# Issuing the routed experts' first token loads behind the shared expert's last load

## The chip, the cores and the metric

The kernel runs on one core of one Trainium2 chip. The core has five engines that run side by side and meet only at semaphores: TensorE (PE in the profile; its weight loads are the row PEld), VectorE (DVE), ScalarE (ACT), GpSimd (POOL) and SyncE (SP). Transfers are started by instructions on SP, ACT or POOL; "SPq" in a row is the queue of transfer instructions that SP works through. The metric is the device time of one execution in microseconds (us), as a median over runs.

## The reference

The computation is four layers in sequence, each one normalizing its input and adding its result to it, on 8 sequences of 512 tokens with 256 channels:

```python
x = x + _L0_attn_ref(_layernorm(x), ...)   # gated recurrence and an MLP
x = x + _L0_ffn_ref(_layernorm(x), ...)    # mixture of experts
x = x + _L1_attn_ref(_layernorm(x), ...)   # gated delta rule
x = x + _L1_ffn_ref(_layernorm(x), ...)    # attention over chosen tokens
```

The change lies in the second layer. Every token goes through one shared expert and through 2 of 8 routed experts, which a softmax over 8 scores picks:

```python
_, idx = jax.lax.top_k(scores + gate_b, 2)
weights = jnp.take_along_axis(scores, idx, axis=-1)
...
h = swiglu((xt @ ew1 + eb1) * (xt @ ew3 + eb3))      # 256 -> 1024 -> 512
acc + ce[:, None] * (h @ ew2 + eb2)                  # 512 -> 256, weighted
...
shared = swiglu((xt @ sw1 + sb1) * (xt @ sw3 + sb3)) @ sw2 + sb2
return (routed + shared)
```

## The kernel before, in words

The four layers are four functions that are traced one after the other: `first_block` (L241), `experts` (L418), `delta_rule` (L566) and `chosen_attention` (L1100). Activations pass between layers through DRAM, in one buffer `xbuf` for each sequence. All arithmetic is in fp32.

`first_block` also routes: for each sequence it leaves the normalized tokens in SBUF (`bz`, eight tiles that stay) and the two chosen experts of every token. `places` (L207) then works out for every token and choice a row of a DRAM buffer `zbuf`, in which tokens of one expert lie together in tiles of 128 rows; there are 71 such tiles.

`experts` has two parts.

**Shared part**, one turn for each of the 8 sequences. `scatter(b)` (L494) issues eight indirect transfers on POOL (L499), each of which writes 128 normalized tokens to their rows of `zbuf`; 64 in all. `shared(b)` (L479) loads the sequence's activations from `xbuf` into the tile `sx` (L481, on SP), turns the normalized tokens with eight transposes (L122), multiplies by the shared weights (L444: 64 matmuls of 128x512), runs the swiglu on ACT and DVE (L448 to L462), adds the bias of the second product to `sx` (L485, on DVE, one instruction), multiplies by the second weights (L490: 32 matmuls), adds that to `sx` (L491) and stores `sx` back to `xbuf` (L492, on SP). There are two `sx` tiles, so the load of sequence n+2 can only follow the store of sequence n.

**Routed part**, one turn for each of the 71 tiles. `fetch(k)` (L504) gathers the tile's expert weights `w` (L508, an indirect transfer on POOL, three buffers), loads its 128 tokens from `zbuf` into `zt` (L510, on SP, three buffers), and turns them (L513, L515). `hidden` and `results` do the matmuls (L444 with the tile `p_r`, L522), and the result is stored to `ybuf` (L525, on SP).

A load of `zt` reads rows of `zbuf` that any scatter may have written, so it waits until the last of the 64 scatters has landed.

The order of the instructions on each engine is not the order of the source. A scheduler puts each engine's instructions into a fixed sequence when the kernel is built, earliest first by its own estimate of when each is ready; on the chip every queue is worked through in that sequence, and an instruction that waits holds up what follows on the same queue. `tc.issue_after(ins)` puts what is traced inside the block behind `ins` in that sequence, for instructions on the same engine as `ins`; it adds no wait for `ins` to finish. The helper `behind` (L527) uses it to put a step of one tile behind the last matmul of the step before. That instruction is on PE, so it orders PE's work alone and says nothing of the loads on SP.

In the kernel before, the queue of SP through this stage reads, in order: store of sequence 2, load of sequence 4, store 3, load 5, the three `zt` loads of tiles 0, 1 and 2, store 4, load 6, store 5, load 7, store 6, the `zt` load of tile 3, store 7, the `zt` load of tile 4, and then stores of `ybuf` and loads of `zt` in turn.

DVE's sequence through this stage has a similar property: L485 of sequence n+1 stands in the middle of the turn of sequence n, between L459 and L449 of that turn.

Of the kernel before, what the change touches and what calls it, by code (L numbers as in the profile page):

```python
# [36 lines left out]
def bc(ap, axis, n):  # L37

    ap = ap.unsqueeze(axis)
    shape = list(ap.shape)  # L40
    shape[axis] = n
    return ap.to_broadcast(shape)
# [3 lines left out]
def block(ctx: ExitStack, tc: tile.TileContext, a: dict, out: bass.AP):  # L46
    nc = tc.nc
# [40 lines left out]
    zbuf = dram.tile([NTILES * TILE, D], F32, name="zbuf")  # L88
    ybuf = dram.tile([NTILES * TILE, D], F32, name="ybuf")

    xbufs = [[dram.tile([T, D], F32, name=f"xbuf{n}_{b}") for b in range(B)] for n in range(2)]


    def rows_of(buf):
        return buf.rearrange("(t p) d -> p t d", p=P)
# [21 lines left out]
    def turn(pool, tag, src, dst, n, weight=None):  # L117

        for c in range(DK):
            pt = pool.tile([P, T], F32, name=f"pt{n}_{c}", tag=tag)  # L120
            for t in range(NT):
                TE.transpose(pt[:, t * P : (t + 1) * P], src[:, t, c * P : (c + 1) * P], ident)  # L122
            if weight is None:
                S.copy(dst[:, c, :], pt)
            else:
                S.activation(dst[:, c, :], pt, AF.Copy, scale=weight[:, c : c + 1])  # L126
# [291 lines left out]
    def experts():  # L418
# [3 lines left out]
        with ExitStack() as cx:  # L422
# [40 lines left out]
                yield  # L463
                return hT

            last_of, hidden_of = [None], [None]

            def whole(gen):

                while True:  # L470
                    try:
                        next(gen)
                    except StopIteration as e:
                        return e.value

            def second(w):
                return w[:, 2 * DK * I2 : WMAT].rearrange("p (f d) -> p f d", d=D)

            def shared(b):  # L479
                x = ch.tile([P, NT, D], F32, name=f"sx{b}", tag="sx")  # L480
                nc.sync.dma_start(x, rows_of(xbufs[0][b]))  # L481
                xT = ch.tile([P, DK, T], F32, name=f"sxT{b}", tag="xT")
                turn(pm, "p1", zs[b], xT, f"s{b}")
                hT = whole(hidden(xT, shared_w, T, f"s{b}"))
                V.tensor_add(x, x, bc(shared_w[:, WMAT + 16 :], 1, NT))  # L485
                w2 = second(shared_w)
                for t in range(NT):
                    ps = po.tile([P, D], F32, name=f"pys{b}_{t}", tag="po")
                    for f in range(4):
                        TE.matmul(ps, hT[:, f, t * P : (t + 1) * P], w2[:, f, :], start=f == 0, stop=f == 3)  # L490
                    V.tensor_add(x[:, t, :], ps, x[:, t, :])  # L491
                nc.sync.dma_start(rows_of(xbufs[0][b]), x)  # L492
# [8 lines left out]
            def tile_rows(buf, k):  # L501
                return buf[k * TILE : (k + 1) * TILE, :]

            def fetch(k):  # L504

                w = ew.tile([P, WROW], F32, name=f"w{k}", tag="w")
                at = bass.IndirectOffsetOnAxis(ap=wrow[:, k : k + 1], axis=0)
                G.indirect_dma_start(w, None, a["experts"].rearrange("e p f -> (e p) f"), at)  # L508
                zt = ch.tile([P, D], F32, name=f"zt{k}", tag="zt", bufs=3)
                nc.sync.dma_start(zt, tile_rows(zbuf, k))  # L510
                pt = po.tile([P, DK, TILE], F32, name=f"ptz{k}", tag="po")
                for c in range(DK):
                    last_of[0] = TE.transpose(pt[:, c, :], zt[:, c * P : (c + 1) * P], ident)  # L513
                zT = ch.tile([P, DK, TILE], F32, name=f"zT{k}", tag="zT")
                S.copy(zT, pt)  # L515
                return w, zT
# [18 lines left out]
            for b in range(B):  # L535
                scatter(b)
                shared(b)


            last_of[0] = None  # L540
            ahead, due = behind(fetch, 0), None
            for k in range(NTILES):
                w, zT = ahead
                work = hidden(zT, w, TILE, f"r{k}")
                next(work)
                for bank in range(4):
                    if bank == 1 and k > 0:

                        with tc.issue_after(hidden_of[0].ins):
                            behind(next, work)  # L550
                    elif bank < 3:
                        behind(next, work)
                    else:
                        hT = behind(whole, work)
                    if bank == 1 and due is not None:
                        behind(results, *due)
                    if bank == 2 and k + 1 < NTILES:
                        ahead = behind(fetch, k + 1)
                due = k, w, hT
            behind(results, *due)  # L560

    experts()
    early.close()

# [827 lines left out]
```

## Time and profile before

| what | value |
|---|---|
| median of 3 runs | 3373.59 us (3373.55 to 3381.02) |
| the profiled execution | 3381.53 us, its span 3379.8 us |
| PE busy over the span | 3018.4 us, 89% |
| DVE, ACT, POOL busy | 56%, 46%, 17% |
| shared part (PE from first to last matmul of it) | about 535 to 847 us |
| routed part | about 847 to 1505 us |
| mean granted clock of TensorE | 0.91 |

The span runs from the first to the last instruction of the profiled execution; its own time is 1.7 us more, and the profile is one execution, so times within it are summed against 3381.53 us and not against the median. Rows of the timeline give a start, a duration, the engine, the line, the operation, and in brackets how long the engine stood idle before it and what ended that. A row with the engine SPq is the short time in which SP issues a transfer, not the transfer.

### The profile page before, as it was taken

What the parts mean: (1) busy time and instruction counts of PE and PEld (TensorE: products, weight loads), DVE (VectorE), ACT (ScalarE), POOL (GpSimd) and SP (SyncE); (2) the same over time, 40 slices, a digit from 0 to 9 for tenths busy, and PEclk for the clock granted to TensorE, in tenths of its full rate; (3) what the DMA queues carried; (4) which work ended last, traced back from release to release, by engine and by line L of the source; (5) the groups of instructions that cost most, each with busy time, mean ns of one, the idle gap of its engine ahead of it and who ended that gap; (6) DMA issues with size and microseconds to landing.
All of it is one profiled execution on the core that took longest, in us unless ns stands there. A gap on an engine that the chain in (4) does not pass through costs nothing.

```text
span 3379.8 us, 59439 instructions
## 1 busy us (share of the span) xinstructions
PE 3018.4 (89%) x24662; PEld 2227.4 (66%) x24662; DVE 1900.5 (56%) x4415; ACT 1548.0 (46%) x2747; POOL 574.0 (17%) x629
## 2 busy tenths in 40 slices
PE   7999999979999999977899898898989999498887
PEld 3655555535999999973566666666666667365664
DVE  4555545534555555556467767767677664554432
ACT  3554442212333333325466666767666663233322
POOL 1000001320000111014122222312121110212111
PEclk8999998989999999998789898989989896698787
DMA  5000003220788888871000000000000000201111
GB/s 205 13 25 13 13 13 148 69 67 19 271 337 330 330 327 320 327 284 31 2 1 20 8 20 8 26 2 26 2 23 2 8 2 8 94 23 42 36 40 47
DMA packets 97133, 302.69 MB, mean 90 GB/s; under 512 B 12760, under 2 KB 79456, under 8 KB 87648
## 3 DMA queue, kind: packets, MB, share of 16 engines
q0 software_dynamic: 19440, 221.19, 17.4%
q1 hardware_dynamic: 68016, 68.44, 6.0%
q10 hardware_dynamic: 9408, 9.27, 0.8%
q8 instruction: 194, 3.18, 0.4%
q14 instruction: 75, 0.61, 0.1%
HBM read 248.79 MB, written 50.08 MB: 88 GB/s over the span
## 4 chain that ended last, share of the span: by engine, by line
PE 69%; DVE 12%; DMA 11%; issue 4%; ACT 2%; POOL 2%; SPq 0%; another core or an unknown queue 0%; ACTq 0%; POOLq 0%; DVEq 0%
PE p_r L444 13%; PE pc L681 8%; DMA zbuf<-bz,rows 5%; PE pp L304 3%; PE pk L746 3%; PE pj L399 3%; PE pyr L522 3%; PE pkq L950 3%; DMA w<-in_experts,wrow 2%; PE pf L394 2%; PE p_s L444 2%; PE py L1008 2%; PE st L1271 2%; PE pw L957 1%; DVE cy L685 1%
## 5 line engine op out<-in xcount | busy, mean ns | idle before, releaser
L444 PE MATMUL p_r<-zT,w 128*128 128x128 f32 x4544 | 533.0, 275 | 6.1 <-DMA w<-in_experts,wrow 5.5
L444 PEld LDWEIGHTS p_r<-zT,w 128*128 128x128 f32 x4544 | 525.0, 192 | 11.6 <-issue 7.1
L685 DVE SCALAR_TENSOR_TENSOR cy<-pc,conv,cy 128x509 f32<-128x509 f32 (+2 forms) x480 | 351.4, 740 | 139.7 <-ACT cy L683 134.6
L448 ACT ACTIVATE t_r<-p_r,w 128x128 f32<-128x128 f32 x568 | 170.9, 374 | 263.5 <-PE p_r L444 183.9
L444 PE MATMUL p_s<-sxT,shared_w 128*128 128x512 f32 x512 | 226.2, 603 | 22.1 <-DVE l_s L449 20.4
L444 PEld LDWEIGHTS p_s<-sxT,shared_w 128*128 128x128 f32 x512 | 98.1, 193 | 145.6 <-issue 106.3
L508 POOL DMA_INDIRECT w<-in_experts,wrow x71 | 66.8, 940 | 676.3 <-ACT sg_r L457 655.8
L449 DVE SCALAR_TENSOR_TENSOR l_r<-p_r,w,t_r 128x128 f32<-128x128 f32 x284 | 80.0, 344 | 175.7 <-PE p_r L444 175.7
L681 PE MATMUL pc<-cxT,wq 128*128 128x512 f32 x256 | 150.8, 714 | 15.0 <-DVE cy L685 12.9
L681 PE MATMUL pc<-cxT,wk 128*128 128x512 f32 x256 | 146.0, 665 | 6.1 <-DVE cy L685 3.7
L304 PE MATMUL pp<-hT,win 128*128 128x512 f32 x320 | 142.9, 598 | 0.2 <-ACT hT L126 0.2
L522 PE MATMUL pyr<-w,htr 128*128 128x256 f32 x568 | 136.0, 383 | 2.6 <-DVE htr L462 2.6
L683 ACT ACTIVATE cy<-pc,conv 128x512 f32<-128x512 f32 x160 | 108.4, 686 | 62.3 <-PE pc L681 61.0
L449 DVE SCALAR_TENSOR_TENSOR g_r<-p_r,w,t_r 128x128 f32<-128x128 f32 x284 | 79.9, 344 | 98.8 <-PE p_r L444 98.8
L746 PE MATMUL pk<-kq 128*128 128x256 f32 x512 | 130.2, 391 | 0.7 <-DVE NQ L748 0.4
L728 POOL TENSOR_TENSOR e<-le,g 128x512 f32<-128x512 f32 x64 | 66.3, 1042 | 364.2 <-DVE NQ L748 341.6
L748 DVE SCALAR_TENSOR_TENSOR NQ<-pk,nbk,e 128x256 f32<-128x256 f32 x256 | 110.0, 477 | 27.2 <-PE pk L746 26.8
L394 PE MATMUL pf<-hT,fc 128*128 128x512 f32 x256 | 121.5, 601 | 0.0
L457 ACT ACTIVATE sg_r<-g_r 128x512 f32<-128x512 f32 x71 | 44.8, 631 | 159.9 <-DVE g_r L455 159.9
L399 PE MATMUL pj<-pj,sT 128*128 128x256 f32 x512 | 113.1, 379 | 0.0
L522 PEld LDWEIGHTS pyr<-w,htr 128*128 128x128 f32 x568 | 103.6, 192 | 14.2 <-issue 2.7
L950 PEld LDWEIGHTS pkq<-state,kq 128*128 128x128 f32 x768 | 95.4, 197 | 24.2 <-DVE state L972 16.7
(393 smaller groups left out, 6179.0 us busy)
## 6 DMA issues: line engine op xcount, KB each, us to landing
zt<-zbuf SPq DMA_DIRECT2D x71, 128.0 KB
ybuf<-yt SPq DMA_DIRECT2D x71, 128.0 KB
zbuf<-zeros SPq DMA_DIRECT2D x11, 768.0 KB
x<-in_x SPq DMA_DIRECT2D x8, 512.0 KB
xbuf<-x SPq DMA_DIRECT2D x8, 512.0 KB
sx<-xbuf SPq DMA_DIRECT2D x8, 512.0 KB
xbuf<-sx SPq DMA_DIRECT2D x8, 512.0 KB
cx<-xbuf SPq DMA_DIRECT2D x8, 512.0 KB
```

The costliest lines, as they stand in the source:

```text
L304: TE.matmul(ps, win[:, k, m : m + P], hT[:, k, :], start=k == 0, stop=k == DK - 1)
L394: TE.matmul(ps, fc[:, k, f * P : (f + 1) * P], hT2[:, k, :], start=k == 0, stop=k == DK - 1)
L399: TE.matmul(ps, sT[:, f, t * P : (t + 1) * P], pj[:, f, :], start=f == 0, stop=f == 7)
L444: last_of[0] = TE.matmul(ps[:, f, :], wx[:, k, (f0 + f) * P : (f0 + f + 1) * P], xin[:, k, :], start=k == 0, stop=k == DK - 1)
L448: S.activation(t3[:, f, :], p3[:, f, :], AF.Identity, bias=b3[:, f0 + f : f0 + f + 1])
L449: V.scalar_tensor_tensor(t1[:, f, :], p1[:, f, :], b1[:, f0 + f : f0 + f + 1], t3[:, f, :], ALU.add, ALU.mult)
L522: last_of[0] = TE.matmul(ps, hT[:, f, :], w2[:, f, :], start=f == 0, stop=f == 3)
L681: TE.matmul(ps, w[:, k, n * P : (n + 1) * P], xT[:, k, :], start=k == 0, stop=k == DK - 1)
L685: V.scalar_tensor_tensor(y[:, j:], ps[:, : T - j], conv[:, at + n, 3 - j : 4 - j], y[:, j:], ALU.mult, ALU.add)
L746: TE.matmul(pk[:, j, :, :], kq[:, h + j, 0, ts], kq[:, h + j, :, ts], start=True, stop=True)
L748: V.scalar_tensor_tensor(NQ[:, :, t * HG + h + j, :], pk[:, j, :, :], s.nbk[:, t, h + j : h + j + 1], bc(e[:, h + j, :], 1, 2), ALU.mult, ...
L950: TE.matmul(ps[:, n, h, :], s.kq[:, h, n, ts], state[:, h, :], start=True, stop=True)
```

## The change

The load of `sx` in `shared` is remembered in `sx_of`, and the load of `zt` in `fetch` is traced inside `tc.issue_after` of the last one remembered, which, when `fetch` runs, is the load of sequence 7.

```diff
-            last_of, hidden_of = [None], [None]
+            last_of, hidden_of, sx_of = [None], [None], [None]
...
                 x = ch.tile([P, NT, D], F32, name=f"sx{b}", tag="sx")
-                nc.sync.dma_start(x, rows_of(xbufs[0][b]))
+                sx_of[0] = nc.sync.dma_start(x, rows_of(xbufs[0][b]))
...
                 zt = ch.tile([P, D], F32, name=f"zt{k}", tag="zt", bufs=3)
-                nc.sync.dma_start(zt, tile_rows(zbuf, k))
+
+                with tc.issue_after(sx_of[0].ins):
+                    nc.sync.dma_start(zt, tile_rows(zbuf, k))
```

In the built kernel the queue of SP then reads: store 3, load 5, store 4, load 6, store 5, load 7, the `zt` loads of tiles 0, 1 and 2, store 6, the `zt` load of tile 3, store 7, and so on as before. These three instructions are all that moves: the sequences of PE, DVE, ACT and POOL are the same, instruction by instruction, and so is the rest of SP's. No transfer is added or taken away, and none changes its size.

## Prediction

> **What bounds the kernel now.** PE is busy 89% of the span, and the chain that ended last is mostly PE, so the kernel is near PE's own work; what can be won is PE's idle time. I read the chain first:
>
> ```profile
> PE 69%; DVE 12%; DMA 11%; issue 4%; ACT 2%; POOL 2%; SPq 0%; another core or an unknown queue 0%; ACTq 0%; POOLq 0%; DVEq 0%
> PE p_r L444 13%; PE pc L681 8%; DMA zbuf<-bz,rows 5%; PE pp L304 3%; PE pk L746 3%; PE pj L399 3%; PE pyr L522 3%; PE pkq L950 3%; DMA w<-in_experts,wrow 2%; PE pf L394 2%; PE p_s L444 2%; PE py L1008 2%; PE st L1271 2%; PE pw L957 1%; DVE cy L685 1%
> ```
>
> The third entry is odd: the scatter to zbuf should feed nothing until the routed part begins, yet 5% of the span (some 170 us) runs through it. Something in the shared part waits for the scatters. The waits of SP and then of PE, over 450 to 1000 us, name both ends of it:
>
> ```profile
> SPq L510 <- DMA zbuf<-bz,rows: 58.7, 1, 58.7
> ...
> PE p_s L444 <- DVE l_s L449: 20.4, 1, 20.4
> ```
>
> SP stands once for 58.7 us at a zt load, for the last scatter; PE stands once for 20.4 us in the shared matmuls. The timeline joins them:
>
> ```profile
> 716.02 0.42 DVE L491 TENSOR_TENSOR sx<-pys,sx 128x256 f32<-128x256 f32 x1 [1.30 <-PE pys L490]
> 717.10 15.72 PE L444 MATMUL p_s<-sxT,shared_w 128*128 128x512 f32 x36 [0.24 <-ACT sxT L124]
> ...
> 722.81 0.69 DVE L459 TENSOR_TENSOR g_s<-g_s,sg_s 128x512 f32<-128x512 f32 x1 [0.69 <-ACT sg_s L457]
> ...
> 740.17 0.96 POOL L499 DMA_INDIRECT zbuf<-bz,rows  x1 [1.74 <-DMA zbuf<-bz,rows]
> 742.60 1.28 SPq L510 DMA_DIRECT2D zt<-zbuf  x3
> 743.98 0.38 SPq L492 DMA_DIRECT2D xbuf<-sx  x1
> 747.49 0.37 SPq L481 DMA_DIRECT2D sx<-xbuf  x1
> 751.28 1.22 DVE L485 TENSOR_TENSOR sx<-sx,shared_w 128x1024 f32<-128x1024 f32 x1 [27.78 <-DMA sx<-xbuf]
> 752.42 0.74 DVE L449 SCALAR_TENSOR_TENSOR l_s<-p_s,shared_w,t_s 128x512 f32<-128x512 f32 x1
> ...
> 753.22 14.47 PE L444 MATMUL p_s<-sxT,shared_w 128*128 128x512 f32 x28 [20.41 <-DVE l_s L449]
> ```
>
> Sequence 4's result is complete at 716.44 (716.02 + 0.42), but its store goes out at 743.98, for the three zt loads stand ahead of it until 742.60. The load of sequence 6, which needs that store's tile, goes at 747.49. DVE has come to L485 for sequence 6 at 723.50 and stands there 27.78 us, with l_s of the running turn behind it; l_s frees PE's PSUM tiles, so PE runs dry at 732.82. Three loads not needed before 846 us have stopped the shared part.
>
> **What the change is worth.** *The stall.* A turn without it lasts 35.96 us: 681.14 to 717.10 with scatters beside it, 775.92 to 811.88 without. The turn of sequence 5 lasts from 717.10 to 775.92, 58.82 us. The difference is **22.86 us**. Two terms are visible: 20.41 us of idle PE, and slow matmuls behind it: the 28 took 14.47 us where 27.73 us for 64, or 0.433 each, would make 12.13, so 2.34 us. 0.1 is left over in the spread of the other rows. The clock column of the windows shows where the 2.34 comes from:
>
> ```profile
> core 0: us, PE busy (x) PEld busy (x) DVE busy (x) ACT busy (x) POOL busy (x), PEclk, DMA share, GB/s
> ...
> 732.82:753.22 20.40, 0.00 (x0) 0.00 (x0) 1.91 (x3) 0.00 (x0) 3.16 (x4) 0.61 0.29 96
> 753.22:755.00 1.78, 1.78 (x2) 0.84 (x3) 1.75 (x3) 0.00 (x0) 0.00 (x0) 0.50 0.00 0
> 755.00:757.00 2.00, 2.00 (x4) 0.88 (x3) 1.27 (x4) 1.49 (x3) 0.00 (x0) 0.50 0.00 0
> 757.00:759.00 2.00, 2.00 (x6) 0.77 (x5) 1.93 (x4) 0.30 (x1) 0.00 (x0) 0.84 0.00 0
> 759.00:761.00 2.00, 2.00 (x6) 0.90 (x5) 1.27 (x3) 1.13 (x2) 0.00 (x0) 1.00 0.00 0
> ```
>
> The granted clock is at half after the pause and whole again near 758. The Trainium skill, "TensorE: Matmul & The Clock Gate", Part 1, says that an idle window halves the clock and that about 3.4 us of work restore it; at half speed that would cost 1.7 us (an estimate), and the sum would be 20.4 + 1.7 = 22.1. The row says 2.34, and I take it: 22.86.
>
> *What is late next.* With the zt loads gone from ahead of it, store 4 goes at 716.5 and load 6 some 3.0 us later (the step 680.51 to 683.54 in the turn before), at 719.5. It lands 3.7 us after issue (747.49 to DVE's release near 751.2): 723.2, against 723.50 when DVE comes to L485. That is tight, but it need not hold: DVE was 27.78 us late and PE lost only 20.41, so about 7.4 us of lateness cost PE nothing. In the turn of sequence 4 the same load, with scatters beside it, made DVE wait for nothing. So a delay up to 7 us costs nothing, and beyond that one for one; I take 0. The same stands for load 7, at 755.4, with the three zt loads directly behind it.
>
> *The scatters.* Store 4 and load 6 now run beside them. In the turn from 644.39 the four scatters beside such a pair took 3.80, 3.75, 3.31 and 3.21 us against 2.66 for an undisturbed one: 3.4 us more. The last scatter lands at about 746.0 instead of 742.6. The cover is what comes next: nobody waits for it before load 7.
>
> *The moved loads.* Store 5 goes when the turn of sequence 5 ends, now at 752.4 (716.44 + 35.96); load 7 follows at 755.4 and the three zt loads to 757. So they are issued 13 us later than before. A rule speaks against that: the Trainium skill, "DMA: Bandwidth & Descriptors", Rules for kernel authors, has a transfer issued early and its semaphore waited for late. By the rule, 13 us of head start are given away. The rows show what they were worth: PE needs tile 0's tokens for the transposes at 846.57, now 823.7, and a zt load of 128 KB cannot take longer than one of sx with 512 KB, 3.7 us, by much. They land by about 762, 62 us in hand: cost 0. If that cover were gone, each us beyond 823.7 would be lost one for one.
>
> *Behind the zt loads* on SP now stands store 6. It is due at 788.4, and the last scatter has landed 42 us before; the zt loads hold it for nothing. Tile 3's load and store 7 stand as before. POOL's and ACT's queues are not passed.
>
> *After the shared part* everything is triggered by what precedes it: the weights of tiles 0 to 2 were gathered at 543 to 555, the fourth is issued when a buffer comes free. PE is busy 646.6 of 653 us there and waits 5.5 us in all for weights, so PE sets the pace and the part starts and ends 22.9 us earlier. The clock was 1.00 in the turns before the stall and in the routed part (847 to 1500), so the pause bought no faster clock that would be given back.
>
> **The sum** against the profiled execution: 3381.53 - 22.86 = 3358.7 us. That execution lies 7.94 us above the median of the runs, and one of the three runs, 3381.02, lies where it does. Carried to the median: 3373.59 - 22.86 = **3350.7 us**, 0.68% less. A measurement of this kernel tells about 0.3%, or 10 us, from no change.
>
> **Rivals.**
>
> *Smaller gain: the stall is shorter without the profiler.* It ends with a chain of 64 scatters, each waiting for another; were each 0.12 us quicker in a plain run, the chain would end 7.9 us sooner, which is the whole gap between the profiled execution and the median. The gain would be 22.86 - 7.94 = 14.9, the time 3358.7. For it: the gap exists. Against: the run of 3381.02 had no profiler. 8%.
>
> *No gain: hidden later.* The routed part might wait at its head for weights or tokens and start at 847 anyway: 3373.6. For it: DMA is at 0.85 there. Against: the first three weights are there 270 us before. 4%.
>
> *Slower: the tokens come too late.* If the scatters, with 512 KB stores and loads now among them, stretched far beyond 3.4 us, the zt loads would hold PE at L513 and store 6 too. From a landing at 846.6 on nothing is won, and slower by over 10 us from 856.7; at 860 the time would be 3373.6 + 13.4 = 3387. The nine scatters that are left at 717 would have to take over 100 us for 25. 3% for any slower end, a worse phase of the clock in the later layers (0.77 to 0.92) among it.
>
> That the change doesn't do what it says is excluded: the built sequence of SP has the three loads behind load 7.
>
> **How the numbers follow.** Forecast 85%, smaller gain 8%, no gain 4%, slower 3%. The range: upward it takes in 3358.7 and the higher of the two levels of runs (3350.7 + 7.5 = 3358.2), with 2 us of margin: 3361. Downward only the 20.4 us term could have been longer in a plain run; 5 us for that: 3345. Faster by over 0.3% is the forecast and the smaller gain, 93%; within 0.3% 4%; slower 3%.
>
> **What would show it.** Right: store 4 at about 716.5 and load 6 at 719.5, no wait of PE for l_s, all turns near 35.96, clock 1.00 throughout the shared part, the last scatter near 746, the zt loads at 755 to 757, and p_r starting at about 824.6. Wrong: a wait of DVE at L485 that reaches PE, an idle PE ahead of L513, or a routed part that begins earlier and ends no earlier.

## The result, and the profile after

The changed kernel takes 3353.26 us (median of 5 runs, 3344.84 to 3361.43) against 3373.59 us before (5 runs, the three of the table above among them, 3373.44 to 3381.02): a ratio of 0.9936, with a 95% interval of 0.9914 to 0.9957. That is 20.3 us less by the medians; 3350.7 was forecast.

The place to look is the turn of sequence 5. The timeline of the changed kernel follows, cut to SP, the matmuls of p_s, the bias and the last scatter; what counts are the starts, and whether a bracket stands behind L485.

```profile
720.04 0.36 SPq L492 DMA_DIRECT2D xbuf<-sx  x1
720.67 27.73 PE L444 MATMUL p_s<-sxT,shared_w 128*128 128x512 f32 x64 [0.24 <-ACT sxT L124]
723.15 0.36 SPq L481 DMA_DIRECT2D sx<-xbuf  x1
727.15 1.23 DVE L485 TENSOR_TENSOR sx<-sx,shared_w 128x1024 f32<-128x1024 f32 x1
747.35 1.16 POOL L499 DMA_INDIRECT zbuf<-bz,rows  x1 [1.73 <-DMA zbuf<-bz,rows]
756.01 0.36 SPq L492 DMA_DIRECT2D xbuf<-sx  x1
756.63 27.73 PE L444 MATMUL p_s<-sxT,shared_w 128*128 128x512 f32 x64 [0.24 <-ACT sxT L124]
758.96 0.36 SPq L481 DMA_DIRECT2D sx<-xbuf  x1
759.37 1.45 SPq L512 DMA_DIRECT2D zt<-zbuf  x3
```

Store 4 goes 0.63 us before the turn's first matmul and not 27 us into it, load 6 3.1 us later, and DVE goes through L485 without a wait. The 64 matmuls run in one row of 27.73 us; before they were two rows with 20.41 us between. The last scatter is issued at 747.35, twelve us before the zt loads want it. Everything here stands 3.57 us later than in the profile before, because the first layer, which is not changed, ended later in this execution.

The windows of the turns of sequences 5, 6 and 7 (busy time of each engine, then the granted clock, the share of DMA and GB/s):

```profile
720.67:756.63 35.96, 35.72 (x105) 19.01 (x105) 17.79 (x29) 8.64 (x15) 9.82 (x9) 1.00 0.21 66
756.63:792.59 35.96, 35.72 (x104) 19.01 (x105) 17.80 (x29) 8.64 (x15) 0.00 (x0) 1.00 0.13 41
792.59:828.12 35.53, 35.07 (x98) 18.35 (x98) 16.65 (x28) 8.38 (x14) 0.00 (x0) 1.00 0.04 15
```

All three are at the undisturbed length and at full clock. The waits of SP and of PE between 450 and 1000 us confirm it by what they no longer have. What is left for PE at p_s, and what the zt loads wait for now:

```profile
PE p_s L444 <- ACT sxT L124: 1.7, 7, 0.2
```

```profile
SPq L512 <- PE ptz L515: 42.6, 4, 35.3
```

Seven waits of 0.2 us for the transposed tokens, as before; and zt loads that wait for a free buffer, not for a scatter (before, that row stood beside the 58.7 us for the scatter, with 41.9 us in 3 waits). The chain of waits, which showed the stall before, is no proof here: its shares by engine add up to under 60%, so in this profile it was followed only through the later part of the span, and an entry that is missing from it says nothing.

The two profiled executions differ by 28.2 us of span (3379.8 and 3351.6), more than the stall. Cut at the starts of four rows, the first matmuls of the shared part, the first and the last of the routed part and the first transposes of the last layer, it comes out so: first layer +4.4, shared part -23.7 (312.0 to 288.3), routed part +0.4, delta rule -6.7 (1420.1 to 1413.4), last layer -2.6. Of the -23.7, 22.86 are the turn of sequence 5 (58.82 to 35.96) and 0.86 the first turn, 37.82 to 36.96, which varied from 36.87 to 38.17 over all kernels run. The rest lies in code that the change does not touch, and the experiments show how far that wanders.

### The profile page after: what moved, and what is told of

The parts are those of the page before. It is cut to its first block, busy times and chain, and to the rows that moved or that the text cites. A ratio compares the mean times of both kernels' runs of the same rounds, so it can differ in the third digit from the quotient of the medians.

```text
span 3351.6 us, 59440 instructions
## 1 busy us (share of the span) xinstructions
PE 3013.0 (90%) x24662; PEld 2225.0 (66%) x24662; DVE 1899.2 (57%) x4415; ACT 1546.6 (46%) x2747; POOL 575.5 (17%) x629
## 4 chain that ended last, share of the span: by engine, by line
PE 38%; DVE 10%; issue 3%; DMA 3%; ACT 2%; POOL 1%; another core or an unknown queue 0%; POOLq 0%; DVEq 0%; ACTq 0%; SPq 0%
PE pc L683 8%; PE pk L748 3%; PE pkq L952 3%; PE py L1010 2%; PE st L1273 1%; PE sc L1252 1%; PE pw L959 1%; PE pg L926 1%; PE pow L978 1%; DVE cy L687 1%; PE pn L878 1%; PE pu L887 1%; PE pn L703 1%; DVE p L795 1%; PE pst L970 1%
## 5 line engine op out<-in xcount | busy, mean ns | idle before, releaser
L750 DVE SCALAR_TENSOR_TENSOR NQ<-pk,nbk,e 128x256 f32<-128x256 f32 x256 | 110.0, 477 | 26.9 <-PE pk L748 26.5
```

The lines of the kernel that those rows point to most:

```text
L750: V.scalar_tensor_tensor(NQ[:, :, t * HG + h + j, :], pk[:, j, :, :], s.nbk[:, t, h + j : h + j + 1], bc(e[:, h + j, :], 1, 2), ALU.mult, ...
```

## The experiments

Twelve runs, in three groups of four kernels; each group ran on one chip, with the kernel before beside it. "Turn" is the time from the first p_s matmul of one sequence to that of the next. The ratios are to the kernel before of the same group, with a 95% interval.

**The change once more.** No edit.

> The changed kernel once more, to see what repeats. The theory (three loads ahead of store 4 on SP stopped DVE at L485 and then PE) expects every turn of the shared part at 35.96 us, as in its first profile, with 22.86 us less than before in the turn of sequence 5, whatever the rest of the span does. The rival, that part of the gain sits elsewhere and only happened to fall so, expects a turn of another length or a stall in another turn. The time: between 3345 and 3361 us, with single runs apart by up to 15 us, from stages that the change does not touch.

3354.11 us (3351.25 to 3356.2), ratio 0.9943 (0.993 to 0.9957). All turns between the first and the last take 35.96 or 35.97 us. What repeats is the turn.

**The three loads on another queue.** The kernel before, with

```diff
-                nc.sync.dma_start(zt, tile_rows(zbuf, k))
+                (G if k < 3 else nc.sync).dma_start(zt, tile_rows(zbuf, k))
```

> The kernel before, but the loads of zt for tiles 0, 1 and 2 are issued by POOL, behind its last scatter, and no load is ordered behind another. The theory expects the whole gain of the change: SP's queue is free, store 4 goes at the end of the turn of sequence 4, all turns last 35.96 us, about 3352 us. The rival that the time of the loads matters (they should not run beside the shared part's own transfers, or are better late) expects less than the gain, for here they go as early as in the kernel before, right after the last scatter at about 746 us.

3349.38 us (3345.66 to 3354.02), ratio 0.9927 (0.9913 to 0.994). All turns 35.96 us. On POOL's timeline the three loads stand right behind the last scatter:

```profile
743.81 1.15 POOL L499 DMA_INDIRECT zbuf<-bz,rows  x1 [1.73 <-DMA zbuf<-bz,rows]
747.01 1.68 POOL L510 DMA_DIRECT2D zt<-zbuf  x3 [2.05 <-PE pys L490]
838.77 1.01 POOL L508 DMA_INDIRECT w<-in_experts,wrow  x1 [90.09 <-ACT sg_r L457]
```

The bracket of the loads names PE, whose result they do not read. They start 3.2 us after the last scatter was issued, as they started 2.4 us after it on SP (740.17 and 742.60 before), so it is taken here that they wait for its landing on POOL too. But what is behind them on POOL has 90 us of time. So neither the transfers nor their early issue were the cost: it was what stood behind them in their queue.

**The bias later on DVE.** The kernel before, SP's order untouched; L485 is put behind the third hidden step of its own turn (cut):

```diff
+                    if f == 2:
+                        thirds.append(hidden_of[0])
...
-                V.tensor_add(x, x, bc(shared_w[:, WMAT + 16 :], 1, NT))
+                with tc.issue_after(thirds[-1].ins):
+                    V.tensor_add(x, x, bc(shared_w[:, WMAT + 16 :], 1, NT))
```

> The kernel before, with SP's order untouched, but DVE adds the bias (L485) late in the sequence's own turn, behind the third of its four hidden steps, instead of in the turn before. The theory says that SP's hold-up reaches PE only through DVE standing at L485: store 4 still goes at about 744 and load 6 at 747.5, but L485 for sequence 6 comes at about 775, after it has landed, so PE loses nothing: turns of 35.96 us, 3350.7 us, as with the change. The rival, that the hold-up costs PE by another way (the tile sx, the clock, the transfers beside it), expects the stall of 20.4 us to stay: 3373.6 us.

3350.84 us (3347.55 to 3357.24), ratio 0.9934 (0.9921 to 0.9948). In this kernel's timeline the bias is L488, the load L483, the store L495, the zt load L513:

```profile
738.71 1.28 SPq L513 DMA_DIRECT2D zt<-zbuf  x3
740.09 0.38 SPq L495 DMA_DIRECT2D xbuf<-sx  x1
741.20 1.22 DVE L488 TENSOR_TENSOR sx<-sx,shared_w 128x1024 f32<-128x1024 f32 x1
743.73 0.37 SPq L483 DMA_DIRECT2D sx<-xbuf  x1
...
777.16 1.22 DVE L488 TENSOR_TENSOR sx<-sx,shared_w 128x1024 f32<-128x1024 f32 x1
```

SP is held up as before: store 4 goes at 740.09, though the turn of sequence 4 had ended before the next one's first matmul at 718.4. That is 21.7 us into the turn, and 26.9 before, for the chain of scatters ended some 5 us earlier in the turn here; by DVE's old place at L485 a stall of about 15 us would still have been left (an estimate: 5.2 us off the 20.4). Yet the turn lasts 35.96 us, for the L488 that needs load 6 comes only at 777.16. With a hold-up on SP that is nearly as long and nothing lost, the way from SP to PE is DVE's place at L485; no other shows. One turn, that of sequence 2, lasted 36.32 us: PE waited 0.3 us for the last hidden tile, which the later bias delays.

**Four scatters fewer.** The kernel before, with

```diff
                         q = b * NT + t
+                        if b == 7 and t >= 2:
+                            continue
```

> The kernel before without the last four of the 64 scatters (half of the tokens of the last sequence do not reach the routed experts, so their output is left out); the order of all else is the same. The theory: the stall ends with the last scatter, so it shortens one for one by 4 x 2.67 = 10.7 us. Store 4 at about 733.3, PE idle 9.7 us instead of 20.4, the turn of sequence 5 lasts 48.1 us, the time is 3373.6 - 10.7 = 3362.9 us. The rival, that something of fixed length (landing of load 6, the clock) makes the stall, expects 20.4 us of idle PE and 3373.6 us.

3360.86 us (3356.33 to 3361.35), ratio 0.9959 (0.9945 to 0.9972). From the timeline (the zt load is L512 here):

```profile
732.15 1.28 SPq L512 DMA_DIRECT2D zt<-zbuf  x3
733.53 0.38 SPq L492 DMA_DIRECT2D xbuf<-sx  x1
736.68 0.37 SPq L481 DMA_DIRECT2D sx<-xbuf  x1
740.46 1.23 DVE L485 TENSOR_TENSOR sx<-sx,shared_w 128x1024 f32<-128x1024 f32 x1 [16.71 <-DMA sx<-xbuf]
742.40 14.91 PE L444 MATMUL p_s<-sxT,shared_w 128*128 128x512 f32 x28 [9.34 <-DVE l_s L449]
```

The same picture as before the change, 11 us shorter: PE idle for 9.34 us (9.7 expected), the turn 48.19 us (48.1 expected).

**Behind the last store.** The change, with the three loads behind store 7:

```diff
-                with tc.issue_after(sx_of[0].ins):
+                with tc.issue_after((store_of if k < 3 else sx_of)[0].ins):
```

where `store_of` holds the last store of `shared` (cut).

> The changed kernel, with the loads of zt for tiles 0, 1 and 2 moved on, behind the store of sequence 7, the last of the shared part. The theory: no turn stalls, but zt of tile 0 is issued only when the last turn has ended, and lands 3 to 5 us later, while PE wants it 0.6 us before that turn's result is complete. So PE waits 4 to 5 us once at L513, ahead of the routed part, and about 1 us of slow clock may follow: 4 to 6 us more than the change, 3358 us. The rival, that the loads are hidden anyway wherever they stand, expects 3353 us and no wait at L513.

3354.29 us (3350.35 to 3361.59), ratio 0.9944 (0.9931 to 0.9958). PE's timeline at the seam to the routed part:

```profile
817.91 7.28 PE L490 MATMUL pys<-shared_w,hts 128*128 128x256 f32 x32
829.32 0.66 PE L515 MATMUL ptz<-ident,zt 128*128 128x128 f32 x2 [4.13 <-DMA zt<-zbuf]
830.45 7.43 PE L444 MATMUL p_r<-zT,w 128*128 128x128 f32 x48 [0.46 <-ACT zT L517]
```

PE waits 4.13 us for the tokens. From the turn's first matmul to the routed part's first it takes 40.11 us instead of 35.53, and the first 48 p_r matmuls take 7.43 us where the same row of other runs has 5.62. Together 4.58 + 1.81 = 6.4 us, slightly over what was expected. The median is 3.7 us under the 3358 expected and lies 4.6 us above that of the run behind load 6, on the same chip; the two intervals overlap, so it is the trace that shows the cost. The loads are not hidden wherever they stand.

**Behind load 6.** The change, one place earlier: every load of `sx` is kept, and the loads of zt are ordered behind the one of sequence 6.

```diff
-                with tc.issue_after(sx_of[0].ins):
+                with tc.issue_after(sx_of[6].ins):
```

> The changed kernel, with the loads of zt one place earlier, behind load 6 (in front of store 5). The theory: the last scatter lands some 29 us into the turn of sequence 5, and store 5 is due at its end, 35.3 us into it; so the hold-up has gone before anybody wants the queue. All turns 35.96 us, 3353 us, the same as the change. The rival, that any store behind the zt loads delays a turn, expects a stall in the turn of sequence 6.

3349.65 us (3347.2 to 3353.72), ratio 0.9938 (0.9924 to 0.9951). All turns 35.96 us. SP's queue in the turn of sequence 5:

```profile
746.76 1.28 SPq L512 DMA_DIRECT2D zt<-zbuf  x3
752.80 0.37 SPq L492 DMA_DIRECT2D xbuf<-sx  x1
```

The zt loads go at 746.76, store 5 behind them at 752.80 when its turn ends: the last of them is issued at 748.04, so there are 4.8 us to spare.

**Eight scatters twice, before.** The kernel before, with

```diff
                 scatter(b)
+                if b == B - 1:
+                    scatter(b)
                 shared(b)
```

> The kernel before with the eight scatters of the last sequence issued twice (the same rows again), so that the last one lands 21.4 us later. The scheduler then puts the zt loads one place later by itself: behind load 6, in front of store 5, as in the run with the loads behind load 6. There the queue was free in time; here the last scatter lands some 50.5 us after the start of the turn of sequence 5. The theory: store 5, due at 35.3, goes at 51.9, load 7 lands at 59.1, DVE is 16.8 us late at L485 in the turn of sequence 6, of which PE can take 7.4: 9.4 us of idle PE in that turn and 2.3 us of slow clock, a turn of 47.6 us, 3365 us. The rival, that what hurts is the place behind load 5 itself, or that it is the load of sequence 6 alone, expects no stall: 3353 us.

3358.75 us (3358.02 to 3359.81), ratio 0.996 (0.9947 to 0.9974): as the scheduler takes the loads of zt one place further back, it is faster than the kernel before with more work in it. From its timeline:

```profile
753.43 15.72 PE L444 MATMUL p_s<-sxT,shared_w 128*128 128x512 f32 x36 [0.24 <-ACT sxT L124]
...
768.23 1.28 SPq L510 DMA_DIRECT2D zt<-zbuf  x3
769.61 0.38 SPq L492 DMA_DIRECT2D xbuf<-sx  x1
772.88 0.37 SPq L481 DMA_DIRECT2D sx<-xbuf  x1
776.77 1.23 DVE L485 TENSOR_TENSOR sx<-sx,shared_w 128x1024 f32<-128x1024 f32 x1 [16.93 <-DMA sx<-xbuf]
778.71 15.07 PE L444 MATMUL p_s<-sxT,shared_w 128*128 128x512 f32 x28 [9.56 <-DVE l_s L449]
```

The stall has moved one turn on, to sequence 6, where it is store 5 and load 7 that are held. DVE waits 16.93 us (16.8 expected), PE 9.56 (9.4), the turn takes 48.59 us (47.6; of the 1 us more, 0.6 is slow clock: the 28 matmuls took 15.07 us, 2.9 over the 12.13 at full clock, where 2.3 was expected). The time is nevertheless 6 us under the 3365 expected, from outside this turn; the spread of the other stages, below, is of that size. The rival that the place behind load 5 is what hurts falls: the run behind load 6 has the same order and no stall, this one the same order and a later last scatter.

**Eight scatters twice, after.** The same edit on the changed kernel.

> The changed kernel with the same eight scatters issued twice. The theory: the zt loads stand behind load 7, so a last scatter at about 50.5 us after the start of the turn of sequence 5 holds up only store 6, which is due at 71.3: nothing is lost, all turns 35.96 us, 3353 us. The rival, that the longer scatters themselves cost PE time by their traffic, expects longer turns, and a loss like that of the kernel before with the doubled scatters.

3346.61 us (3345.7 to 3347.8), ratio 0.9925 (0.9911 to 0.9938). All turns 35.96 us. SP's queue:

```profile
756.71 0.36 SPq L481 DMA_DIRECT2D sx<-xbuf  x1
772.64 1.28 SPq L512 DMA_DIRECT2D zt<-zbuf  x3
789.64 0.37 SPq L492 DMA_DIRECT2D xbuf<-sx  x1
```

The zt loads go 16 us after load 7, and store 6 behind them when it is due. The longer scatters cost the turns nothing by themselves.

**Four kernels without a stall, side by side.** The change, the loads on POOL, the loads behind load 6, and the change with doubled scatters once more, on one chip.

> The changed kernel beside three other kernels without a stall, on one chip. The shared part is the same to 0.1 us in all of them, so the theory expects the same time, with medians of five apart by no more than about 5 us: that the run with the loads on POOL (3349.4 us), with doubled scatters (3346.6) and the change itself (3354.1) differed is the spread of the other stages. The rival: one of these places really is better, and then its median is the lowest here again.

> The loads of tiles 0 to 2 on POOL, as before. The theory: the change's time within 5 us, about 3351 us. The rival: again some 5 us below the change.

> The loads of tiles 0 to 2 behind load 6, as before. The theory: the change's time within 5 us, about 3351 us. The rival: below the change by more than that.

> The changed kernel with eight scatters issued twice, as before. The theory: the change's time within 5 us, about 3351 us. The rival: again the lowest, some 7 us below the change, though it does more work than any other.

| kernel | median, us | range, us | ratio to before (95%) | turn of sequence 5 |
|---|---|---|---|---|
| the change | 3347.74 | 3345.11 to 3348.36 | 0.9929 (0.9917 to 0.9942) | 35.96 |
| loads on POOL | 3343.57 | 3339.55 to 3346.97 | 0.9918 (0.9905 to 0.9931) | 35.96 |
| loads behind load 6 | 3349.63 | 3344.64 to 3358.39 | 0.9937 (0.9924 to 0.995) | 35.96 |
| change, doubled scatters | 3346.08 | 3340.54 to 3355.03 | 0.9929 (0.9917 to 0.9942) | 35.96 |

The medians are 6 us apart, a little more than was expected, and the order is not that of the run before: the doubled scatters are no longer ahead. The loads on POOL had the lower median both times, by 4.7 and 4.2 us against the change on the same chip. The intervals overlap and the shared parts are alike (289.2 and 289.5 us), so whether that is a gain, which its rival expected, and where it would come from, stays open. The profiles do not settle it: with the loads on POOL the routed part was 2.7 us shorter in this group and 0.3 in the first, and the delta rule behind it 3.4 and 0.9 us longer. It is surely faster than the kernel before, and not surely faster than the change.

## Why the prediction was right

*The chain SP, DVE, PE.* Both ends were broken by themselves: the loads on POOL took SP's hold-up away, the late bias left most of it in place and cut it off from PE, and both took the stall away whole. Four scatters fewer shortened the turn by 10.6 us (10.7 expected), and eight more made the stall that was expected one turn later. This is shown. Not tested by itself is the step between, that load 6 needs the tile of store 4: load 6 stands behind the zt loads on SP in any case, so a third `sx` tile alone, with the order kept, would, by that order, not have freed it. The tile's own share is small: load 6 goes 3.5 us after store 4 (743.98 to 747.49).

*The size.* 22.86 us was expected from the turn, and the turn of sequence 5 went from 58.82 to 35.96: the number itself. The medians differ by less, 20.3, and in the two later groups by 20.5 and 23.9. These differences stand on both sides of the forecast. That they come from stages outside the turn is read from the profiles, for the timed runs have no stages: over fourteen profiles the turns between the first and the last agree to 0.4 us wherever nothing stalls, while the delta rule took 1408.2 to 1420.1 us and the last layer 447.2 to 457.5, the profile before being the longest in both. The turn was forecast; that a median of five, from single runs 16.6 us apart, fell within 3 us of 3350.7 is in part luck.

*The smaller gain without a profiler* (14.9 us) falls: three groups of timed runs give 20 us and more, and the interval of the third, up to 0.9942, leaves no gain under 19.6 us (those of the first two, up to 0.9957, would leave 14.5). The gap of 7.94 us between the profiled execution and the median was put down to a possible shorter chain of scatters; that execution had the longest delta rule and the longest last layer of all that were profiled, by 4.1 and 2.6 us over the next, which is nearly the gap.

*The slack of DVE.* It was read as 27.78 - 20.41 = 7.4 us that PE can take. Both new stalls give the same: 16.71 - 9.34 and 16.93 - 9.56 are 7.37. In the profile before, PE runs on for 9.32 us after DVE has come to L485 (723.50 to 732.82), on the PSUM tiles that are still free; once the load has landed, DVE needs 1.94 us for L485 and the l_s behind it until PE goes on (751.28 to 753.22). The difference, 7.38, is the slack, and it was the same in the three turns that stalled.

*The moved pieces*, taken 3.57 us earlier for comparison: store 4 at 716.47 (716.5 predicted), load 6 at 719.58 (719.5), the zt loads from 755.80 (755.8), p_r from 824.55 (824.6), the last scatter landed, 2.4 us after its issue, at about 746.2 (746.0).

*The head start of the loads.* By the rule to issue early 13 us of head start were given away; the change lost nothing by it, and the loads on POOL and behind load 6, which got it back, show a turn of the same length. The other end exists too: behind store 7 the loads come 4.13 us late.

*The slow clock behind the pause.* The term of 2.34 us was measured; the estimate by the rule was 1.7. The new stalls speak for measuring: 28 matmuls took 14.91 us and 15.07 us there, so 2.8 and 2.9 us over the 12.13 at full clock, behind pauses of about half the length. The step of the estimate that was short is the length of the slow time, 3.4 us: read from the clock column it was 4.4 us here and 5.3 and 5.6 us behind the new stalls, and half of each, 2.2, 2.7 and 2.8, is the loss to within 0.15 us. The last section shows why it varies.

*No gain* and *slower* needed a wait at the head of the routed part. PE's waits show none beyond 0.5 us there.

## What to carry to other kernels

In this kernel a transfer that waited on SP held everything behind it, so look for each long wait on a transfer queue at what stands behind it and when that is due; the cost is that delay less the slack of whoever waits in the end, and a stretch of slow clock behind it. It shrinks with the delay (11 us less of it, 11 us less idle PE, with four scatters fewer) and is nothing once the wait ends before the next one in the queue is due. The same loads cost 22.86 us in front of store 4, nothing in front of store 5 or store 6, and 6.4 us behind store 7; with a last scatter some 21 us later they cost 12.6 us in front of store 5 too. So a place in the queue is good or bad only against the time at which the wait ends. A wait can cross two engines before it shows: PE was shown waiting for DVE, which waited for a load that waited for a store that waited behind a load nobody needed for 100 us.

## What was not expected of the hardware

A short pause of TensorE is dear. In the run behind store 7 it was idle for 4.12 us, and the clock was halved within that pause (its mean granted clock is 0.77) and stayed so for some 5 us after it. The run with the stall in the turn of sequence 6 has it after 9.56 us. Its windows of PE (busy time, granted clock, share of DMA, GB/s):

```profile
769.15:778.71 9.56, 0.00 (x0) 0.76 0.47 151
778.71:780.00 1.29, 1.29 (x2) 0.50 0.00 0
780.00:782.00 2.00, 2.00 (x3) 0.50 0.00 0
782.00:784.00 2.00, 2.00 (x4) 0.50 0.00 0
784.00:786.00 2.00, 2.00 (x6) 0.91 0.00 0
```

The clock is whole again at about 784.4, 5.6 us after the first matmul. Over four pauses of 4.12, 9.34, 9.56 and 20.41 us the time at half clock afterwards, read so, was 5.0, 5.3, 5.6 and 4.4 us: it does not grow with the pause. The 4.13 us for which PE waited behind store 7 thus cost 6.4. No shorter pause was measured.

The times of the changes say more. Read from windows of 0.5 to 2 us, each mean between 0.5 and 1 placing one change, the clock was halved at 827.44 and whole again at 834.27 in the run behind store 7, at 737.48 and 747.72 with four scatters fewer, at 774.12 and 784.36 here, and at 737.18 and 757.66 before: 6.83, 10.24, 10.24 and 20.48 us apart, which are 2, 3, 3 and 6 times 3.41 us. Six further changes in the profile before, between 1501.76 and 1549.55, lie whole multiples of 3.41 us from 757.66, to within 0.01. So in these traces the clock changes only on a fixed grid of 3.41 us, and where a pause falls on it decides what it costs: the halving came 2.2 to 5.0 us into the pause, and the half clock outlasted the pause by more than one step and less than two. Half of that, 1.7 to 3.4 us, is what a pause would add for matmuls that fill PE (an estimate from these figures; 2.3 to 2.9 was measured).
